# Gate products of one attention stage: thirteen queries in one product, or twelve as two products in the two halves of the TensorE rows

## The chip, the core and the metric

The kernel runs on one core of a Trainium2 chip. The metric is the device time of one execution in microseconds (us). Four compute engines work from queues of their own and in order: PE (TensorE, matrix products into PSUM), DVE (VectorE), ACT (ScalarE) and POOL (GpSimd). SP (SyncE) issues the DMAs. An engine that waits for a semaphore holds up everything behind it in its queue. PSUM has eight banks per partition, each of 512 fp32 numbers. All data here is fp32.

An fp32 matrix product appears in the trace as two passes, each with a weight load (row PEld) and a MATMUL (row PE). A PE transpose is one pass.

## What is computed

The program is a block of two layers: gated cross-attention, a batch attention with a mixture of experts, a second cross-attention and a spiking network. The change concerns the first stage alone, cut here to what it touches:

```
emb  = [sin(mul), cos(mul)],  mul = 100 * log(box relations) * (1, 1000^-1/2)    # per query, key
g    = relu(emb @ Wg.T + bg)                                    # a gate per head, query, key
a    = q @ k.T / sqrt(64)
mn   = softmax(log(clip(g, 1e-6)) + a)
out  = (mn @ v) @ Wo.T + bo
x    = x + tanh(g_xattn[0]) * out
```

There are 8 batches of 512 queries and 512 keys, 16 heads of 64. The gate of a head, a query and a key is a product over 16 features: sines and cosines of box distances in x and y, which depend on the query and the key together, and of box widths and heights, which split into a query factor and a key factor.

## The kernel before

**Tiling.** The stage runs over 32 steps (`NSTEP`), each of 128 queries of one batch against all 512 keys. A step has eight pairs of heads (`p` = 0 to 7). While step `i` does its attention, the gates of step `i + 1` are computed, and the features of steps `i + 2` and `i + 3`.

**Gates (`gate_half`, L436).** The 128 queries are cut into ten blocks of `QB` = 13 (the last has 11). A half is one block with two of the four key tiles: two products that contract over `GR` = 116 rows and give 128 keys by 13 x 16 = 208 gates. The stationary operand is a slice of `emb` (key features), the moving one a slice of `wst` (gate weights, with the query factors written in). The rows are 52 cosine features, 8 products and one bias, a gap, and 52 sine features from row 64. Each half has a PSUM tile `pg` of one bank, of which there are two (`bufs=2`). It is then copied into `gates` by DVE in `p` = 0, 2 and 7, by ACT in the others (L455). A step has 20 halves; `HALVES` says how many belong to each pair.

**Order.** PE, ACT and DVE are in `manual_schedule`: in the loop over steps they run in the order in which the code names the work. For a pair `p` it is: `scores(i, p + 1)`, a half, `weigh(i, p)`, a half, `values(i, p - 1)`, a half, then outputs and features.

- `scores` (L460): two products of 64 rows each, one per head, in the upper and the lower half of the PE rows and each with a bank of its own (`pS`, L469). DVE takes the row maximum (`nm`, L473), then ACT two exponentials (`e`, L476).
- `weigh` (L479): eight transposes of `e` into `pT` (L485), and one DVE instruction that multiplies by the gates (`at`, L487).
- `values` (L492): eight products with `v` into `po` (L505); after every second pair DVE divides (L511, L513).
- `outputs` (L518) transposes the result, `mix` (L530) multiplies it by `Wo` once per step, in `p` = 2 (L536).

**Features.** They live in `lt` and `nt`, on 116 partitions by 5 x 512 numbers, 26 queries per tile. For a later step DVE does `offsets` (`p` = 4, 5), `clip` (6), `turns` (0), `whole`, `rest` (1) and `rest_sizes` (2); ACT does `sizes` (5), `log` (7) and `sines` (2). In `p` = 3 `place` moves them into `emb` with four DMAs (L361), and `load_products` adds the product rows. `load_keys` brings key coordinates once per batch with four DMAs. All of these DMAs are issued from SP, in one queue with the loads of `kT` (L419) and `v` (L425), which are issued three pairs (`kT`) and two pairs (`v`) ahead of their use.

PSUM is full: `pg` 2 banks, `pS` 2, `pT` 2, `po` 1, and 1 for the outputs.

Of the kernel before, what the change touches and what calls it, by code (L numbers as in the profile page):

```python
# [12 lines left out]
F32 = mybir.dt.float32  # L13
# [7 lines left out]
P = 128  # L21
B, S, D = 8, 512, 256
NT = B * S // P
NQ = S // P
# [45 lines left out]
            )  # L70


QB = 13
NB = 10
GR = 64 + 4 * QB
PAIRS = H // 2
MANUAL = {mybir.EngineType.PE, mybir.EngineType.Activation, mybir.EngineType.DVE}

# [194 lines left out]
def gated_cross_attention(cx, a, tg, x1q, d, front):  # L273
# [2 lines left out]

    tc, nc, ident = cx.tc, cx.nc, cx.ident
    NSTEP = B * NQ
    NP = NB // 2
    with ExitStack() as es:  # L280
        cp = es.enter_context(tc.tile_pool(name="xc", bufs=1))
        cx.halfpi = cp.tile([P, 1], F32, name="halfpi")
        nc.gpsimd.memset(cx.halfpi, math.pi / 2)
        crow = cp.tile([P, 1], F32, name="crow")
        wo = cp.tile([P, PAIRS, D], F32, name="wo")
        wst = [cp.tile([P, P * H], F32, name=f"wst{k}") for k in range(2)]
        embs = [cp.tile([P, NP, 2, S], F32, name=f"emb{k}") for k in range(2)]
        for e in embs:
            nc.gpsimd.memset(e, 0.0)
        kd = cp.tile([P, 2, S], F32, name="kd")  # L290
        nc.gpsimd.memset(kd, 0.0)
        qs = cp.tile([P, NSTEP * NP], F32, name="qs")
        qi = cp.tile([P, NSTEP * NP], F32, name="qi")
        lt = cp.tile([P, NP, S], F32, name="lt")
        nt = cp.tile([P, NP, S], F32, name="nt")

        def load_keys(b):
            for r0 in (0, 2 * QB, 64, 64 + 2 * QB):
                nc.sync.dma_start(
                    out=kd[r0 : r0 + 2 * QB, b % 2, :],  # L300
                    in_=d["kc"][2 * b + (1 if r0 % 64 else 0)].partition_broadcast(2 * QB),
                )

        def load_products(j):


            nc.sync.dma_start(
                out=wst[j % 2][4 * QB : 4 * QB + 8, :].rearrange("j (q h) -> j q h", h=H),
                in_=d["qx"][:, j * P : (j + 1) * P, :],
            )  # L310
            if j % NQ < 2:
                nc.sync.dma_start(
                    out=embs[j % 2][4 * QB : 4 * QB + 9].rearrange("j a t k -> j (a t) k"),
                    in_=d["kx"][j // NQ // 4, :, j // NQ % 4 * S : (j // NQ % 4 + 1) * S].unsqueeze(1).to_broadcast([9, NB, S]),
                )

        R = slice(0, GR)

        def offsets(j, t0, t1):
            for t in range(t0, t1):
# [33 lines left out]

        def place(j):

            for src, r0 in ((lt, 0), (nt, 64)):
                for half in range(2):  # L360
                    nc.sync.dma_start(  # L361
                        out=embs[j % 2][r0 : r0 + 4 * QB, :, half, :],
                        in_=src[64 * half : 64 * half + 4 * QB],
                    )

        def features(j, *fns):
            for fn in fns:
                if 0 <= j < NSTEP:
                    fn(j)

        with ExitStack() as pro:
            batch = project_all(cx, a, d, pro)
            bp = pro.enter_context(tc.tile_pool(name="bq", bufs=1))
            box = box_terms(cx, a, d, pro)
            bx = bp.tile([P, NSTEP * NP, 2], F32, name="bx")
            nc.sync.dma_start(out=bx, in_=a["boxq"])
            nc.sync.dma_start(out=crow, in_=a["crow"])
            nc.vector.tensor_tensor(qs, bx[:, :, 0], bx[:, :, 1], ALU.add)
            nc.vector.tensor_scalar(qs, qs, 0.5, None, ALU.mult)
            nc.vector.tensor_tensor(qi, bx[:, :, 1], bx[:, :, 0], ALU.subtract)  # L380
            nc.vector.tensor_scalar(qi, qi, 1.0, None, ALU.add)
            nc.vector.reciprocal(qi, qi)
            for b in range(B):
                xnT = batch(b)
                box(b)
                if b == 0:
                    load_keys(0)

                if b < 4:
                    w, cols = wst[b // 2], slice(b % 2 * 8 * P, (b % 2 + 1) * 8 * P)  # L390
                    nc.gpsimd.tensor_copy(w[0:1, cols][:, 0:1], xnT[0:1, 0, 0:1])
                    nc.sync.dma_start(out=w[0:GR, cols], in_=a["wst"][:, cols])
                if b in (4, 5):
                    w = wo[:, 4 * (b - 4) : 4 * (b - 3), :]
                    nc.gpsimd.tensor_copy(w[0:1, 0, 0:1], xnT[0:1, 0, 0:1])
                    nc.sync.dma_start(out=w, in_=a["woT"][:, 4 * (b - 4) : 4 * (b - 3), :])
                if b == 6:
                    bo = cx.bcast(cp, a["bo"], "bo")
                if b in (1, 3, 5):
                    j = b // 2  # L400
                    offsets(j, 0, NP)
                    features(j, sizes, clip, log)
                if b in (2, 4):
                    j = b // 2 - 1
                    load_products(j)
                    features(j, turns, whole, rest, rest_sizes, sines, place)
# [8 lines left out]
        def load_key(i, p):  # L415
            i, p = i + p // PAIRS, p % PAIRS
            if i < NSTEP:
                kTs[i, p] = wk.tile([P, S], F32, name="kT", tag="kT", bufs=3)
                nc.sync.dma_start(out=kTs[i, p], in_=d["k"][i // NQ, p])  # L419
# [12 lines left out]
        def load_rest(i):  # L432
            xts[i] = wk.tile([P, D], F32, name="xt", tag="xt", bufs=1)
            nc.sync.dma_start(out=xts[i], in_=a["x"][i * P : (i + 1) * P, :])

        def gate_half(i, k, copy):  # L436


            if i == NSTEP:
                return  # L440
            blk, hf = divmod(k, 2)
            if k == 0:
                gates[i] = big.tile([P, H, NQ, P], F32, name="gate", tag="gate")
            q0 = blk * QB
            nq = min(QB, P - q0)
            pg = ps.tile([P, 2, 256], F32, name="pg", tag="g", bufs=2)
            for c in range(2):
                kc = 2 * hf + c
                nc.tensor.matmul(  # L449
                    pg[:, c, 0 : nq * H],  # L450
                    embs[i % 2][R, blk // 2, blk % 2, kc * P : (kc + 1) * P],
                    wst[i % 2][R, q0 * H : (q0 + nq) * H],
                    start=True, stop=True,
                )
            copy(  # L455
                gates[i][:, :, 2 * hf : 2 * hf + 2, q0 : q0 + nq].rearrange("p h k q -> p k h q"),
                pg[:, :, 0 : nq * H].rearrange("p k (q h) -> p k h q", h=H),
            )

        def scores(i, p):  # L460
# [85 lines left out]

        HALVES = (3, 3, 3, 2, 2, 2, 2, 3)
        SINES, LOG = 2, 7  # L550

        for p in range(3):
# [8 lines left out]
        with tc.manual_schedule(engines=MANUAL):  # L561
            for i in range(NSTEP):
                k = 0
                for p in range(PAIRS):
# [4 lines left out]
                    def half():  # L569
                        if halves:  # L570
                            gate_half(i + 1, halves.pop(0), copy)

                    if p == 0:
                        load_queries(i + 1)
                        if (i + 3) % NQ == 0:
                            features(i + 3, lambda j: load_keys(j // NQ))
                    load_key(i, p + 3)
                    scores(i, p + 1)
                    if p == SINES:
                        features(i + 2, rest_sizes, sines)  # L580
                    if p == LOG:
                        features(i + 3, log)
                    half()
                    weigh(i, p)
                    half()
                    values(i, p - 1)
                    load_value(i, p + 2)
                    half()
                    if p in (3, 5, 7):
                        outputs(i, (p - 3) // 2)  # L590
                    if p == 1:
# [8 lines left out]
                        features(i + 2, load_products, place)  # L600
                        load_rest(i)
                    if p == 4:
                        features(i + 3, lambda j: offsets(j, 0, 3))
                    if p == 5:
                        features(i + 3, lambda j: offsets(j, 3, NP), sizes)
                    if p == 6:
                        features(i + 3, clip)
                    if i == NSTEP - 1:
# [1161 lines left out]
def _gate_layouts(boxes, wg, bg):  # L1770


    ntile = B * NQ * (NB // 2)
    boxq = np.zeros((P, ntile, 2), np.float32)
    crow = np.zeros((P, 1), np.float32)
    wst = np.zeros((GR, P, H), np.float32)
    flat = boxes.reshape(B * NQ, P, 4)
    for half in range(2):
        for t in range(NB // 2):
            q = np.minimum(np.arange(QB) + (2 * t + half) * QB, P - 1)  # L1780
            for c in range(2):
                for f in range(2):
                    r0 = 64 * half + (2 * c + f) * QB
                    crow[r0 : r0 + QB] = _turns(f)
                    for e in range(2):
                        boxq[r0 : r0 + QB, t :: NB // 2, e] = flat[:, q, c + 2 * e].T
    for q in range(P):
        for c in range(2):
            for f in range(2):
                r = (2 * c + f) * QB + q % QB  # L1790
                wst[r, q] = wg[:, 2 * c + f]
                wst[64 + r, q] = wg[:, 8 + 2 * c + f]
    wst[4 * QB + 8] = bg

    sc = np.stack([wg[:, 4:8], wg[:, 12:16]]).transpose(2, 0, 1)
    wext = np.stack([sc[:, ::-1], sc])
    return {
        "boxq": boxq,
        "boxc": boxes.reshape(B, S, 2, 2).transpose(0, 3, 2, 1).reshape(2 * B, 2, S),
        "boxt": boxes.reshape(NT, P, 4).transpose(1, 0, 2),  # L1800
        "crow": crow,
        "wst": wst.reshape(GR, P * H),
        "wext": wext.reshape(2 * P),
    }

# [73 lines left out]
```

## Time and profile before

The median of three runs is 2934.63 us (2933.69 to 2938.61). The profiled execution took 2940.68 us, of which the span of the trace is 2938.9 us.

| stretch of the trace, us | PE busy | DVE busy | ACT busy | clock |
|---|---|---|---|---|
| projections, 0 to 354 | 341.13 | 125.06 | 120.42 | 1.00 |
| gates of the first step, 354 to 380 | 22.43 | 8.16 | 9.63 | 1.00 |
| 50 us inside the 32 steps, 1000 to 1050 | 49.83 | 37.38 | 30.31 | 1.00 |
| the rest, 1950 to 2938.9 | 943.39 | 529.43 | 347.24 | 0.96 |

PE busy counts a MATMUL from its start to its modelled end, so passes overlap in it; "idle before" of a group is the time in which its engine had nothing running before an instruction of the group, and the arrow names what ended it. "Clock" is the granted TensorE clock. In the stage of the steps (about 380 to 1950 us) the clock is 1.00 throughout.

### The profile page before, as it was taken

The numbers are of one execution on the slowest core, as the hardware profiler recorded it, in microseconds if no ns is written. First come the engines' busy times: TensorE is split into PE (matmuls) and PEld (weight loads), VectorE is DVE, ScalarE is ACT, GpSimd is POOL, SyncE is SP. The second block draws the span as 40 slices with busy tenths as digits, with TensorE's granted clock in tenths as the row PEclk, the third lists the DMA queues.
The fourth block names the chain that finished last, engine by engine and source line by source line (L and its number), as shares of the span: only waits on it lengthen the run. The fifth ranks groups of instructions, "written<-read, shape, count | busy, mean of one in ns | idle before, by whom it ended". The sixth has DMA issues, their size and how long they took to land.

```text
span 2938.9 us, 39143 instructions
## 1 busy us (share of the span) xinstructions
PE 2866.8 (98%) x15188; PEld 2095.2 (71%) x15188; DVE 1826.5 (62%) x2862; ACT 1404.0 (48%) x2196; POOL 138.4 (5%) x138
## 2 busy tenths in 40 slices
PE   8999999999999999999999999999999998999998
PEld 3444478888888888888888888877775665456566
DVE  6432177777777777777777767557862112566757
ACT  4332256566666666656565665435541121343434
POOL 2000000000000000000000000000002111212100
PEclk9999999999999999999999999999998998999999
DMA  7775545555555555454546464443113333111100
GB/s 226 220 227 188 180 119 155 142 155 142 150 152 146 156 140 158 135 163 131 166 131 167 131 166 129 134 128 140 47 55 129 129 127 107 58 44 57 29 15 22
DMA packets 270105, 381.84 MB, mean 130 GB/s; under 512 B 55048, under 2 KB 136840, under 8 KB 267104
## 3 DMA queue, kind: packets, MB, share of 16 engines
q1 hardware_dynamic: 266848, 370.95, 43.9%
q0 software_dynamic: 3072, 8.39, 1.0%
q8 instruction: 120, 1.97, 0.3%
q14 instruction: 65, 0.53, 0.1%
HBM read 237.23 MB, written 73.88 MB: 106 GB/s over the span
## 4 chain that ended last, share of the span: by engine, by line
PE 79%; DVE 13%; issue 2%; DMA 2%; ACT 1%; SPq 0%; POOL 0%; ACTq 0%; DVEq 0%; POOLq 0%
PE pg L449 13%; PE po L505 11%; PE pS L469 7%; PE pT L485 6%; PE pk L226 6%; PE ph L1525 4%; PE pw L536 4%; PE ph L1308 4%; PE py L1317 4%; PE py L1540 4%; PE pv L241 3%; DVE nm L473 2%; PE pz L1497 2%; DVE lt L346 2%; PE pq L700 2%
## 5 line engine op out<-in xcount | busy, mean ns | idle before, releaser
L476 ACT ACTIVATE e<-pS,nm 128x512 f32<-128x512 f32 x512 | 324.3, 684 | 576.4 <-DVE nm L473 576.0
L449 PE MATMUL pg<-wst,emb 116*128 116x208 f32 (+1 forms) x2560 | 581.5, 350 | 8.1 <-DVE gate L455 5.8
L449 PEld LDWEIGHTS pg<-wst,emb 116*128 116x128 f32 x2560 | 414.1, 189 | 205.2 <-issue 79.8
L505 PEld LDWEIGHTS po<-v,at 128*128 128x128 f32 x4096 | 493.0, 192 | 0.1
L505 PE MATMUL po<-v,at 128*128 128x65 f32 x4096 | 485.7, 272 | 0.0
L473 DVE TENSOR_REDUCE nm<-pS 128x2 f32<-128x1024 f32 x256 | 312.5, 1221 | 176.2 <-PE pS L469 176.2
L487 DVE SCALAR_TENSOR_TENSOR at<-gate,pT 128x1024 f32<-128x1024 f32 x256 | 311.1, 1215 | 46.4 <-PE pT L485 45.4
L469 PE MATMUL pS<-kT,qT 64*128 64x512 f32 x1024 | 291.2, 641 | 5.6 <-ACT e L476 2.0
L485 PE MATMUL pT<-ident,e 128*128 128x128 f32 x2048 | 266.4, 273 | 0.0
L485 PEld LDWEIGHTS pT<-ident,e 128*128 128x128 f32 x2048 | 239.8, 141 | 13.9 <-DVE o L513 1.5
L455 DVE COPY gate<-pg 128x416 f32<-128x416 f32 (+1 forms) x289 | 164.6, 570 | 51.2 <-PE pg L449 30.9
L455 ACT COPY gate<-pg 128x416 f32<-128x416 f32 x351 | 166.7, 531 | 33.6 <-PE pg L449 31.2
L1321 DVE TENSOR_TENSOR ye<-py,b 128x256 f32<-128x256 f32 x32 | 13.6, 424 | 208.0 <-PE py L1317 208.0
L1312 ACT ACTIVATE hT<-ph,eb 128x512 f32<-128x512 f32 x64 | 44.0, 687 | 177.7 <-PE ph L1308 171.9
L226 PE MATMUL pk<-ctxT,wk__121 128*128 128x512 f32 x256 | 114.9, 604 | 11.2 <-DMA ctxT<-in_ctxT 7.6
L63 POOL TENSOR_TENSOR ln_rs<-ln_ve,mhalf 128x4 f32<-128x4 f32 (+1 forms) x25 | 25.5, 1019 | 2050.5 <-DVE ln_ve L62 1990.3
L1525 PE MATMUL ph<-xnT,wf 128*128 128x512 f32 (+2 forms) x320 | 118.7, 513 | 1.8 <-ACT xnT L1393 1.5
L536 PE MATMUL pw<-wo,oT 128*128 128x256 f32 x512 | 117.6, 383 | 0.5 <-ACT oT L528 0.5
L241 PE MATMUL pv<-wv,ctxT 128*128 128x512 f32 x256 | 114.7, 593 | 1.0 <-DVE vs L245 1.0
L1308 PE MATMUL ph<-dT,w 128*128 128x512 f32 x256 | 111.9, 595 | 2.7 <-DVE dT L1293 2.1
L469 PEld LDWEIGHTS pS<-kT,qT 64*128 64x128 f32 x1024 | 77.8, 184 | 51.1 <-issue 36.4
L226 PE MATMUL pk<-xnT,wq 128*128 128x512 f32 x256 | 113.0, 594 | 0.6 <-DVE xnT L261 0.6
(252 smaller groups left out, 3910.7 us busy)
## 6 DMA issues: line engine op xcount, KB each, us to landing
v<-vdr SPq DMA_DIRECT2D x256, 260.0 KB
kT<-kdr SPq DMA_DIRECT2D x256, 256.0 KB
emb<-lt SPq DMA_DIRECT2D x64, 520.0 KB
emb<-nt SPq DMA_DIRECT2D x64, 520.0 KB
vdr<-vs SPq DMA_DIRECT2D x8, 2080.0 KB
kdr<-st SPq DMA_DIRECT2D x64, 256.0 KB
qdr<-st SPq DMA_DIRECT2D x64, 256.0 KB
qT<-qdr SPq DMA_DIRECT2D x32, 512.0 KB
```

Source lines behind the costliest of these rows:

```text
L226: nc.tensor.matmul(pk, w[:, c, m * P : (m + 1) * P], src[:, c, :], start=(c == 0), stop=(c == 1))
L449: nc.tensor.matmul(pg[:, c, 0 : nq * H], embs[i % 2][R, blk // 2, blk % 2, kc * P : (kc + 1) * P], wst[i % 2][R, q0 * H : (q0 + nq) * H], ...
L455: copy(gates[i][:, :, 2 * hf : 2 * hf + 2, q0 : q0 + nq].rearrange("p h k q -> p k h q"), pg[:, :, 0 : nq * H].rearrange("p k (q h) -> p k ...
L469: nc.tensor.matmul(pS[:, t, :], qTs[i][rows, p, :], kT[rows, :], start=True, stop=True)
L473: nc.vector.tensor_reduce(nm, pS, AX.X, ALU.max, negate=True)
L476: nc.scalar.activation(e[:, t, :], pS[:, t, :], AF.Exp, bias=nm[:, t : t + 1])
L485: nc.tensor.transpose(pT[:, t, kc, :], e[:, t, kc * P : (kc + 1) * P], ident)
L487: nc.vector.scalar_tensor_tensor(at, gates[i][:, 2 * p : 2 * p + 2], 1e-6, pT, ALU.max, ALU.mult)
L505: nc.tensor.matmul(po[:, 2 * (p % 2) + t, :], at[:, t, kc, :], v[:, kc, t, :], start=(kc == 0), stop=(kc == NQ - 1),)
L536: nc.tensor.matmul(pw, oT[:, c, :], wo[:, c, :], start=(c == 0), stop=(c == PAIRS - 1))
L1308: nc.tensor.matmul(ph, w1[:, c, f * P : (f + 1) * P], dT[:, c, :], start=(c == 0), stop=(c == 1),)
L1525: nc.tensor.matmul(ph[:, 0:n], wf[:, c, f * P : (f + 1) * P], xnT[:, c, tok], start=(c == 0), stop=(c == 1),)
```

## The change

The block becomes twelve queries: six in rows 0 to 56 of PE and six in rows 64 to 120 (`QB` = 6, `GR` = 57). `g` counts these two row halves: `g` = 0 holds queries 0 to 63 of the step, `g` = 1 queries 64 to 127. A half is now four products of 57 rows and 6 x 16 = 96 columns, in the order c = 0: g = 0, g = 1; c = 1: g = 0, g = 1. There are 11 blocks, so 22 halves in a step; the last block has 4 queries per row half. `pg` is one tile `pgs` of two banks for the whole stage: each row half has its bank, and inside each bank the first 256 columns belong to halves with `hf` = 0, the others to `hf` = 1.

The order in a pair becomes: a half, `scores`, a half, a half, `weigh`, `values`. Features are computed on 128 partitions by 4 x 512 numbers; `place` takes 20 DMAs in place of 4, `load_keys` 12 in place of 4, and `load_products` twice as many.

```diff
-QB = 13
-NB = 10
-GR = 64 + 4 * QB
+HQ = P // 2
+QB = 6
+NB = 11
+GR = 8 * QB + 9
+NS = P // (4 * QB)
...
         def place(j):
...
-            for src, r0 in ((lt, 0), (nt, 64)):
-                for half in range(2):
+            for src, r0 in ((lt, 0), (nt, 4 * QB)):
+                for s in range(NS):
+                    rows = src[4 * QB * s : 4 * QB * (s + 1)]
+                    for g in (s // 2,) if s < 4 else (0, 1):
+                        b0, n = (4 * (s % 2), 4) if s < 4 else (8, 2)
+                        nc.sync.dma_start(
+                            out=embs[j % 2][64 * g + r0 : 64 * g + r0 + 4 * QB, b0 : b0 + n, :],
+                            in_=rows[:, 0:4, :] if s < 4 else rows[:, 2 * g : 2 * g + 2, :],
+                        )
+                for t in range(4):
+                    at = 64 * (t // 2) + r0 + 8 * (t % 2)
                     nc.sync.dma_start(
-                        out=embs[j % 2][r0 : r0 + 4 * QB, :, half, :],
-                        in_=src[64 * half : 64 * half + 4 * QB],
+                        out=embs[j % 2][at : at + 8, NB - 1, :], in_=src[4 * QB * NS :, t, :]
                     )
...
+        pgs = ps.tile([P, 2, 2, 2 * P], F32, name="pg", tag="g")
+
         def gate_half(i, k, copy):
...
-            nq = min(QB, P - q0)
-            pg = ps.tile([P, 2, 256], F32, name="pg", tag="g", bufs=2)
+            nq = min(QB, HQ - q0)
+            pg = pgs[:, :, hf, 0 : 2 * nq * H].rearrange("p g (k n) -> p g k n", k=2)
             for c in range(2):
                 kc = 2 * hf + c
-                nc.tensor.matmul(
-                    pg[:, c, 0 : nq * H],
-                    embs[i % 2][R, blk // 2, blk % 2, kc * P : (kc + 1) * P],
-                    wst[i % 2][R, q0 * H : (q0 + nq) * H],
-                    start=True, stop=True,
-                )
+                for g in range(2):
+                    rows = slice(64 * g, 64 * g + GR)
+                    nc.tensor.matmul(
+                        pg[:, g, c, :],
+                        embs[i % 2][rows, blk, kc * P : (kc + 1) * P],
+                        wst[i % 2][rows, q0 * H : (q0 + nq) * H],
+                        start=True, stop=True,
+                    )
...
-        HALVES = (3, 3, 3, 2, 2, 2, 2, 3)
+        HALVES = (3, 3, 3, 2, 2, 3, 3, 3)
...
                     load_key(i, p + 3)
+                    half()
                     scores(i, p + 1)
                     if p == SINES:
                         features(i + 2, rest_sizes, sines)
                     if p == LOG:
                         features(i + 3, log)
                     half()
+                    half()
                     weigh(i, p)
-                    half()
                     values(i, p - 1)
                     load_value(i, p + 2)
-                    half()
...
                     if p == 4:
-                        features(i + 3, lambda j: offsets(j, 0, 3))
+                        features(i + 3, lambda j: offsets(j, 0, 2))
                     if p == 5:
-                        features(i + 3, lambda j: offsets(j, 3, NP), sizes)
+                        features(i + 3, lambda j: offsets(j, 2, NP), sizes)
```

## The prediction, made before the changed kernel ran

> **What bounds the kernel now.** First the page, then windows, a timeline inside the steps, and the rows of the groups. PE runs without a gap from 380 to 1950 us (49.83 of 50 us busy in the window from 1000), and the chain of waits names PE for most of the span:
>
> ```profile
> PE 79%; DVE 13%; issue 2%; DMA 2%; ACT 1%; SPq 0%; POOL 0%; ACTq 0%; DVEq 0%; POOLq 0%
> ...
> L449 PE MATMUL pg<-wst,emb 116*128 116x208 f32 (+1 forms) x2560 | 581.5, 350 | 8.1 <-DVE gate L455 5.8
> ...
> L738 PE MATMUL pS<-qkT 64*128 64x128 f32 x256 | 23.9, 307 | 0.0
> ```
>
> The gate products wait 8.1 us in all. The third row, from the batch attention, has the form that the change gives them. One pair of heads, p = 6 (columns: start, us, engine, line):
>
> ```profile
> 1009.95 1.13 PE L469 MATMUL pS<-kT,qT 64*128 64x512 f32 x4
> ...
> 1011.01 0.97 PE L449 MATMUL pg<-wst,emb 116*128 116x208 f32 x4
> 1011.19 1.22 DVE L473 TENSOR_REDUCE nm<-pS 128x2 f32<-128x1024 f32 x1 [1.45 <-PE pS L469]
> ...
> 1011.81 1.04 PE L485 MATMUL pT<-ident,e 128*128 128x128 f32 x8
> ...
> 1012.57 1.26 ACT L476 ACTIVATE e<-pS,nm 128x512 f32<-128x512 f32 x2
> ...
> 1012.69 0.87 PE L449 MATMUL pg<-wst,emb 116*128 116x208 f32 x4
> ...
> 1013.39 1.90 PE L505 MATMUL po<-v,at 128*128 128x65 f32 x16
> 1013.70 0.96 ACT L455 COPY gate<-pg 128x416 f32<-128x416 f32 x2
> ```
>
> Read it thus: PE is full, and ACT copies both gate halves only after the exponentials, 2.7 us after the first half starts and 1.0 after the second. That costs nothing, since a half waits for the copy of two halves earlier: each has its own tile. L469 starts the pairs p = 3, 4, 5, 6, 7, 0, 1, 2 at 993.67, 999.17, 1004.45, 1009.95, 1015.22, 1021.26, 1027.30, 1033.55, and p = 3 again at 1043.42: a step is 49.75 us.
>
> **What the change takes off PE.** Starts of single passes: a gate pass comes each 0.175 us, so 18 halves of 4 passes (0.70) and two narrower (0.59) are 13.8 us a step. In L738, passes of the two row halves start 7 ns apart, and a pair of passes each 0.107 to 0.112, the same as L505 with 65 columns: a pass costs its weight load there, so 96 columns won't beat it. A new half, four pairs of passes, is 0.44; 22 are 9.6. **PE saves 4.2 us a step.** Were the row halves not concurrent: 19.2, a loss of 5.4.
>
> Other edits. DVE feature rows sum to 11.5 us a step (L324 5 x 0.54; L333 1.48, L339 1.54, L342 1.49, L346 2.82, L82 1.48): a fifth, 2.3, goes; of ACT's four at 2.34, 1.9 goes. ACT gains two copies (+1.0). All lies beside PE, except where it stands before a copy (below). Copies of 384 instead of 416 numbers: 0.50 ACT, 0.55 DVE. `place`: 4 issues of 0.87 become 20 of some 0.33 (estimate, as kT's 0.32 to 0.43), +3.1 us on SP; the queued kT and v loads are over 9 us ahead of use, which hides it; uncovered it would cost 3 us a step. `load_keys` has 8 more issues per batch: under 1 us a step, same cover. Switches between whole-row and half-row products (0.2 us between passes instead of 0.11) stay at two a pair.
>
> **The wait it adds.** `pgs` holds both halves in the same two banks. In the program as built, each half waits for the copy of the half just before it; in the old one, of two before. The Trainium skill ("PSUM — Partial Sum Buffer", section "PSUM bank collisions raise a hardware error") says to guard PSUM by bank, not by address, as an engine reading a bank collides with PE writing elsewhere in it. So this wait belongs to the layout: by address two halves are free and 4.2 us are gained; by bank there is one buffer. No run here shows a collision; the waits in the program decide.
>
> And the new order puts halves B and C together behind the scores. Walk p = 6, t = 0 where half A starts on PE:
> - A 0 to 0.54 (first weight load exposed, 0.11, as in L738); results 0.75. Copy A on ACT 2.2 to 2.7 (behind `sizes`); pS 0.54 to 1.40.
> - nm starts 1.13 after pS starts (trace above, less the switch): 1.67 to 2.89. Exponentials 2.93 to 4.19, behind copy A.
> - B may start at 2.75; copy B stands behind the exponentials on ACT: 4.2 to 4.73. **C waits for it: 4.78 to 5.32.**
> - Queued behind C on PE: transposes 5.42 to 6.40, `values` to 8.19, next A at 8.3. Before: 5.27.
>
> The same for each pair, PE at clock 1.00, then at 0.50 (every PE duration doubled, DVE and ACT unchanged):
>
> | p | before | clock 1.00 | clock 0.50 | what ends the wait |
> |---|---|---|---|---|
> | 3 | 5.50 | 6.05 | 9.8 | next A: copy B behind table load and exponentials |
> | 4 | 5.28 | 4.80 | 9.4 | none |
> | 5 | 5.50 | 8.7 | 13.4 | C: copy B behind exponentials; nm 0.2 late behind offsets |
> | 6 | 5.27 | 8.3 | 13.0 | as walked |
> | 7 | 6.04 | 8.1 | 12.2 | B: copy A behind clip (to 2.5); C: copy B behind nm (4.3) |
> | 0 | 6.04 | 7.0 | 11.7 | C: copy B behind nm (3.5) |
> | 1 | 6.25 | 8.9 | 13.4 | C: as p = 6, nm 0.4 late behind turns |
> | 2 | 9.87 | 13.3 | 18.1 | B: copy A behind whole and rest (3.2); C: copy B behind nm, rest_sizes (6.2) |
> | sum | 49.75 | 65.15 | 101.0 | |
>
> At clock 1.00 a step costs +15.4; 31 steps have halves: +477. The first step's 22 halves stand alone: each 0.75 to the copy, 0.53 copy, 0.05: 1.33, 29 us plus scores, against 23.6: +7. Sum on the profiled run: 2940.7 + 484 = **3425**.
>
> **The clock.** C's wait leaves PE idle for up to 2.9 us in a row. Here is what idling did to the clock elsewhere in this trace (window, us, PE busy, PEld, DVE, ACT, POOL, clock):
>
> ```profile
> 1974.61:1978.02 3.41, 1.53 (x16) 1.17 (x14) 3.31 (x6) 0.10 (x1) 0.00 (x0) 1.00 0.53 150
> 1978.02:1981.43 3.41, 2.97 (x13) 1.91 (x14) 2.03 (x10) 3.09 (x11) 1.01 (x1) 0.50 0.78 90
> ...
> 2216.95:2220.37 3.42, 3.42 (x18) 3.42 (x17) 0.25 (x1) 0.00 (x0) 0.00 (x0) 0.50 0.00 0
> ```
>
> 1.53 us busy in a stretch of 3.41, and the next stretch is at half clock; and at 2216.95 passes of 32 columns, back to back, do not bring it back. I counted, per stretch of 3.41 us (the grid on which the clock changes), the share in which columns stream (0.83 ns a column of a product, half that for a transpose): the clock fell after stretches with 0.00 to 0.29 (eight; one of 0.26 kept it; all others at full clock had 0.35 or more), stayed low up to 0.75, and rose from 0.82 on. The Trainium skill ("TensorE: Matmul & The Clock Gate", section "HAM oscillation — how this bites in real kernels") asks only for no idle gap above some 3.4 us. By that rule 2.9 us are harmless and the sum stays 3425. By the rows, a stretch that begins 0.75 to 3.5 us into p = 5, 6 or 1 streams under 0.29: 2.75 of 3.41, 80% of phases. I take the rows.
>
> At low clock a pair streams about half its time (`values` 65 of 128 columns' time), too little to rise, until `mix` in p = 2 (6.9 us of full streaming). So p = 3 and 4 run at full clock, p = 5 falls near its end (11.5), p = 6, 7, 0, 1 are low, and in p = 2 mix ends at full clock: 6.05 + 4.80 + 11.5 + 13.0 + 12.2 + 11.7 + 13.4 + 18.1 = 90.8. With a fifth of the falls one pair late and a short rise now and then: 88. 31 x (88 - 49.75) = 1186, the first step +10: 2940.7 + 1196 = 4137 for the profiled run. The median lies 6 us lower: **4130**.
>
> **Rivals.**
> - Clock stays up: 3425. For it: no idle gap reaches 3.4 us; against: the windows above. 0.17.
> - Falls, but rises often in p = 7 or 0: 3500 to 3850. 0.15.
> - Faster: the waits hide, and PE keeps its 4.2 us: 2940 - 31 x 4.2 = 2810. It needs all waits of a step under 4.2 us, 0.5 at each C; a copy alone is 0.5. For it: DVE is idle for a quarter of the step, ACT for two fifths; against: their order is fixed, and it puts the exponentials before copy B. 0.04.
> - Smaller waits than walked: 2945 to 3300. 0.04.
> - Row halves run one after the other: up to 0.44 more per half, +300 at full clock; inside the range with the forecast. L738 speaks against.
>
> The forecast has 0.60, with 3850 to 4350 as its own range. 3380 to 4350 adds the middle case and half of the first rival: about 0.8. 0.2% (6 us) is what a measurement can tell from no change: faster 0.04, same 0.01, slower 0.95.
>
> **What shows it.** The pg group (5632 passes) has hundreds of us idle before it, ended by gate copies of both engines; B to C apart by exponentials or nm; pass pairs 0.11 apart at clock 1.00; clock digits of 5 to 8 in the steps' slices. Wrong if the group's idle stays near 8 us, or the clock at 9.

## The result, and the profile after

The changed kernel takes **3879.78 us** (median of four runs, 3875.76 to 3896.08) against 2936.62 us for the kernel before in the same comparison: a ratio of **1.3218**, interval 1.3173 to 1.3264. The profiled execution took 3882.64 us, its span is 3880.9 us, and the mean granted clock is 0.807.

The first view is again the page: the chain of waits, the row of the gate products, and the row of the scores, which wait for keys.

```profile
PE 68%; DVE 12%; ACT 5%; SPq 4%; issue 2%; DMA 2%; POOL 0%; DVEq 0%; ACTq 0%; POOLq 0%
...
L468 PE MATMUL pg<-wst,emb 57*128 57x96 f32 x5632 | 605.5, 347 | 424.4 <-ACT gate L474 272.8
...
L489 PE MATMUL pS<-kT,qT 64*128 64x512 f32 x1024 | 364.4, 793 | 13.1 <-DMA kT<-kdr 12.5
```

The gate products now wait 424.4 us (8.1 before), mostly for copies by ACT. Their busy time (the time in which at least one of their passes runs) did not fall (605.5 against 581.5 us), although a pass has 96 columns in place of 208. The 942.0 us that the span has gained divide on PE like this: PE busy went from 2866.8 to 3378.7 us (+511.9), and PE idle from 72.1 to 502.2 us (+430.1), of which the gate products are 416.3.

The timeline of one pair, p = 5 (columns: start, us, engine, line), shows both:

```profile
1079.39 0.69 PE L468 MATMUL pg<-wst,emb 57*128 57x96 f32 x8
...
1079.91 1.05 PE L489 MATMUL pS<-kT,qT 64*128 64x512 f32 x4
...
1080.80 0.59 PE L468 MATMUL pg<-wst,emb 57*128 57x96 f32 x8
...
1081.31 1.22 DVE L493 TENSOR_REDUCE nm<-pS 128x2 f32<-128x1024 f32 x1
1082.56 1.27 ACT L496 ACTIVATE e<-pS,nm 128x512 f32<-128x512 f32 x2 [1.96 <-DVE nm L493]
1083.72 0.48 ACT L474 COPY gate<-pg 128x384 f32<-128x384 f32 x1
...
1084.25 1.17 PE L468 MATMUL pg<-wst,emb 57*128 57x96 f32 x8 [2.86 <-ACT gate L474]
...
1085.35 1.97 PE L505 MATMUL pT<-ident,e 128*128 128x128 f32 x8
...
1087.11 3.51 PE L525 MATMUL po<-v,at 128*128 128x65 f32 x16
```

The three L468 rows are halves A, B and C. B is done at 1081.4, but its copy stands on ACT behind `nm` and both exponentials; C starts 2.86 us late. C's own eight passes then take 1.17 us where A's took 0.69, the transposes 1.97 (1.04 before), the values 3.51 (1.90 before): that is the clock at half. The windows of the same stretch (us, then busy time of PE, PEld, DVE, ACT, POOL, then clock, DMA share, GB/s) show when it went:

```profile
1076.83:1080.25 3.42, 3.42 (x34) 3.24 (x34) 2.62 (x4) 1.77 (x4) 0.00 (x0) 1.00 0.27 74
1080.25:1083.66 3.41, 1.13 (x12) 0.56 (x8) 2.14 (x3) 1.45 (x3) 0.00 (x0) 1.00 0.59 130
1083.66:1087.07 3.41, 2.82 (x16) 2.65 (x17) 0.00 (x0) 1.02 (x3) 0.00 (x0) 0.50 0.68 173
...
1090.49:1093.90 3.41, 3.41 (x17) 1.70 (x18) 0.00 (x0) 2.58 (x3) 0.00 (x0) 0.50 0.89 261
1093.90:1097.31 3.41, 0.91 (x16) 0.74 (x16) 1.23 (x1) 1.64 (x3) 0.00 (x0) 1.00 0.78 251
```

The stretch with C's wait holds 1.13 us of PE work, and the next one is at 0.50. At 1093.90 the clock is back for one stretch, and the wait for copy B of p = 6 takes it away again.

Where the 942 us lie along the run, by the starts of the gate and mix passes: up to the first gate product +10.8, gates of the first step +20.9 (44.0 against 23.1), the 32 steps **+913.4** (2496.8 against 1583.3), everything behind them -3.2. The clock over the steps' stretch is 0.72, behind it 0.97 (0.96 before).

### The profile page after: what moved, and what is told of

Same layout as the page of the kernel before. It is cut to its first block, busy times and chain, and to the rows that moved or that the text cites. A ratio compares the mean times of both kernels' runs of the same rounds, so it can differ in the third digit from the quotient of the medians.

```text
span 3880.9 us, 46550 instructions
## 1 busy us (share of the span) xinstructions
PE 3378.7 (87%) x18260; PEld 2524.8 (65%) x18260; DVE 1777.4 (46%) x2831; ACT 1385.9 (36%) x2259; POOL 139.3 (4%) x137
## 4 chain that ended last, share of the span: by engine, by line
PE 68%; DVE 12%; ACT 5%; SPq 4%; issue 2%; DMA 2%; POOL 0%; DVEq 0%; ACTq 0%; POOLq 0%
PE po L525 14%; PE pg L468 9%; PE pT L505 8%; PE pS L489 7%; DVE nm L493 6%; PE pw L556 4%; ACT e L496 3%; PE ph L1545 3%; PE ph L1328 3%; PE py L1337 3%; PE py L1560 3%; SPq L371 2%; PE pk L228 2%; PE pz L1517 1%; SPq L377 1%
## 5 line engine op out<-in xcount | busy, mean ns | idle before, releaser
L468 PE MATMUL pg<-wst,emb 57*128 57x96 f32 x5632 | 605.5, 347 | 424.4 <-ACT gate L474 272.8
L468 PEld LDWEIGHTS pg<-wst,emb 57*128 57x128 f32 x5632 | 511.6, 245 | 710.8 <-ACT gate L474 396.7
L525 PEld LDWEIGHTS po<-v,at 128*128 128x128 f32 x4096 | 699.5, 265 | 0.1
L525 PE MATMUL po<-v,at 128*128 128x65 f32 x4096 | 697.9, 343 | 0.0
L505 PE MATMUL pT<-ident,e 128*128 128x128 f32 x2048 | 403.5, 360 | 0.0
L474 ACT COPY gate<-pg 128x384 f32<-128x384 f32 x414 | 199.2, 481 | 494.8 <-PE pg L468 492.4
L489 PE MATMUL pS<-kT,qT 64*128 64x512 f32 x1024 | 364.4, 793 | 13.1 <-DMA kT<-kdr 12.5
L505 PEld LDWEIGHTS pT<-ident,e 128*128 128x128 f32 x2048 | 318.1, 184 | 36.1 <-issue 18.5
L474 DVE COPY gate<-pg 128x384 f32<-128x384 f32 (+1 forms) x290 | 152.4, 525 | 235.8 <-PE pg L468 235.8
L556 PEld LDWEIGHTS pw<-wo,oT 128*128 128x128 f32 x512 | 131.8, 265 | 26.4 <-ACT oT L548 0.7
```

The costliest lines, as they stand in the source:

```text
L468: nc.tensor.matmul(pg[:, g, c, :], embs[i % 2][rows, blk, kc * P : (kc + 1) * P], wst[i % 2][rows, q0 * H : (q0 + nq) * H], start=True, st ...
L474: copy(gates[i][:, :, 2 * hf : 2 * hf + 2, :] .rearrange("p h k (g q) -> p g k h q", g=2)[:, :, :, :, q0 : q0 + nq], pg.rearrange("p g k ( ...
L489: nc.tensor.matmul(pS[:, t, :], qTs[i][rows, p, :], kT[rows, :], start=True, stop=True)
L505: nc.tensor.transpose(pT[:, t, kc, :], e[:, t, kc * P : (kc + 1) * P], ident)
L525: nc.tensor.matmul(po[:, 2 * (p % 2) + t, :], at[:, t, kc, :], v[:, kc, t, :], start=(kc == 0), stop=(kc == NQ - 1),)
L556: nc.tensor.matmul(pw, oT[:, c, :], wo[:, c, :], start=(c == 0), stop=(c == PAIRS - 1))
```

## The experiments

Two theories: the shared banks and the copy's place behind the exponentials make PE wait, and the waits lower the clock (the forecast's); or the loss comes from something else in the change: the row halves, the order of the pair, or `place` with its twenty DMAs. Each ratio is to the kernel before in the same comparison (2937.8 to 2938.8 us).

### One row half alone, with a buffer each

Gates of queries 64 to 127 are not computed; each half has its own bank, two in turn, as in the kernel before.

```diff
-        pgs = ps.tile([P, 2, 2, 2 * P], F32, name="pg", tag="g")
...
+            pgt = ps.tile([P, 512], F32, name="pg", tag="g", bufs=2)
...
-                for g in range(2):
+                for g in range(1):
```

> The order, the copies and the features of the changed kernel, but only the products of row half 0 are done (the gates of queries 64 to 127 are left out; each copy reads the same 192 numbers twice), and each half has a bank of its own, two in turn. The pitch of the passes stays that of the weight load, so PE has the same time to fill. Theory 'one buffer' (both halves lie in the same two banks, so a half waits for the copy of the half just before): the waits go, idle before the gate products falls from 424 us to under 40, the clock stays above 0.97 and the time is near 2940 - 31 x 4.2 = 2810 (2770 to 2900). Rival 'order' (the new place of the halves, all in front of the transposes, is what stalls PE): waits stay, over 3300. Rival 'half rows' (57-row products keep the clock low by themselves): no waits but a clock under 0.9, over 3200.

Measured: 3690.24 us, ratio 1.2559 (1.2397 to 1.2721), clock 0.78. A miss: 880 us above the expected 2810. The gates' wait did go (27.7 us in the 96-column products, 389.7 in the changed kernel), but the timeline from p = 5 into p = 6 shows what stood behind it:

```profile
1030.00 4.87 SPq L371 DMA_DIRECT2D emb<-nt  x6
...
1034.91 2.67 SPq L377 DMA_DIRECT2D emb<-nt  x4
...
1038.12 0.42 SPq L434 DMA_DIRECT2D kT<-kdr  x1
...
1040.91 2.08 PE L488 MATMUL pS<-kT,qT 64*128 64x512 f32 x4 [6.28 <-DMA kT<-kdr]
```

SP is still issuing `place` (L371, L377) when a quick step needs its next keys; `kT` is issued at 1038.12, and PE waits 6.28 us, once per step, 194.0 us in all. After it the four score passes take 2.08 us: half clock again. Such a wait does not keep the clock at 0.78 by itself: with both row halves, a kernel further down waits 202 us for keys in the same way, at a clock of 0.94. What else is slow here comes up with the second version of this kernel.

### The order of the pair

First, the order of the kernel before, with the shared banks of the change (`scores`, a half, `weigh`, a half, `values`, a half):

```diff
-                    half()
                     scores(i, p + 1)
...
-                    half()
                     weigh(i, p)
+                    half()
                     values(i, p - 1)
                     load_value(i, p + 2)
+                    half()
```

> The changed kernel with the old order of a pair (scores, half, transposes, half, values, half); the shared banks stay. 'One buffer': half 2 waits for copy 1, which ACT does behind the exponentials, but PE has the transposes in between, so 1.6 us of wait a pair are left instead of 2.9, and idle stretches are too short to lower the clock often: about 3300 (3150 to 3500), clock above 0.9. Rival 'order': 2800 to 2950, as the old order is back.

Measured: 3706.03 us, ratio 1.2613 (1.257 to 1.2656), clock 0.85; gates wait 318 us. Setting the order back recovers 174 of 943 us. The order is a small part of the cause, and the waits with one buffer cost more than expected in either order (the time is 206 us above the range).

Then only the queue on ACT is changed: `exponents` split off from `scores` and named behind half B, so that copy B runs before the exponentials.

```diff
                     scores(i, p + 1)
+                    half()
+                    exponents(i, p + 1)
...
                     half()
-                    half()
                     weigh(i, p)
```

> The changed kernel, with one thing moved on ACT: the two exponentials come behind the copy of the second half instead of in front of it. Banks and order of PE stay. 'One buffer' with the queue on ACT as what makes the wait long: in the pairs with ACT copies C waits 0.7 us (latency and copy) instead of 2.9; the pairs with DVE copies keep theirs (copy B behind the row maximum). Steps near 56 us, time about 3140 (3000 to 3300), clock above 0.95. If the exponentials were not what holds the copy: unchanged, 3880.

Measured: 3545.98 us, ratio 1.2068 (1.1907 to 1.2229), clock 0.88. 334 us come from the place of the exponentials alone; the range was missed by 246 us. Groups of this kernel by line and shape:

```profile
L468 PE MATMUL pg<-wst,emb 57*128 57x96 f32 x5120 | 481.2, 312 | 189.3 <-DVE gate L474 128.0 <-ACT gate L474 60.4 <-issue 0.9
L489 PE MATMUL pS<-kT,qT 64*128 64x512 f32 x1024 | 335.6, 733 | 166.6 <-DMA kT<-kdr 164.6 <-DMA v<-vdr 1.5 <-ACT e L503 0.5
```

The gates' wait for ACT fell from 272.3 to 60.4 us, and the keys' wait rose from 12.5 to 164.6: the same `place` in SP's queue.

### Filling the wait

To part the wait from the clock, PE gets useless work where it waits: four products of 64 x 512 between B and C, their result overwritten, in pairs with three halves.

```diff
                     half()
+                    if halves and i + 1 < NSTEP:
+                        fill(i)
                     half()
```

> The changed kernel with work added: in each pair of three halves PE does four more products of 64 rows by 512 columns between half B and half C (1.7 us at full clock, into the transposes' banks, overwritten by them; the results are not used). 'Idle lowers the clock': they fill the wait, the clock stays above 0.95 and the time falls to that of the walk at clock 1.00, 3350 to 3430, though PE does 27 us... 31 x 6 x 1.7 = 316 us more work. Rival 'the clock is low for another reason' (half-row products, few columns): clock stays near 0.8, 3880 or more.

Measured: **3508.33 us**, ratio 1.194 (1.1878 to 1.2002), 80 us above the top of the expectation, and 371 us *faster* than the changed kernel. The group of the added products:

```profile
L506 PE MATMUL pT<-qT,ident 64*128 64x512 f32 x1488 | 423.9, 694 | 0.0
```

PE runs these products for 423.9 us (the time in which at least one of them runs), and the mean clock is 0.952 instead of 0.807. The eight transposes of a pair take 1.09 us again. This run shows that PE's low clock in the changed kernel is due to its idling, not to the products in row halves as such.

### `place` by itself

The kernel before, with nothing changed but `place` cut into twenty DMAs:

```diff
-                    nc.sync.dma_start(
-                        out=embs[j % 2][r0 : r0 + 4 * QB, :, half, :],
-                        in_=src[64 * half : 64 * half + 4 * QB],
-                    )
+                    for t in range(NP):
+                        nc.sync.dma_start(
+                            out=embs[j % 2][r0 : r0 + 4 * QB, t, half, :],
+                            in_=src[64 * half : 64 * half + 4 * QB, t, :],
+                        )
```

> The kernel before, with place alone changed: the same bytes in 20 DMAs instead of 4. 'Two waits': SP is held some 11 us longer, the kT load of pair 7 comes about 6 us late in each step, PE stands still and the clock falls for some pairs: 3100 to 3500. Rival 'hidden' (my prediction's line: kT and v are loaded over 9 us ahead, so nothing is lost): 2935 to 2950.

Measured: 3102.9 us, ratio 1.0559 (1.0534 to 1.0584). The listing of the DMA's line (ns, smallest, median, largest) and the groups:

```profile
L362 SPq DMA_DIRECT2D emb<-lt x320: 743/755/1547, 75.3 to 2010.0; - x160
L362 SPq DMA_DIRECT2D emb<-nt x320: 743/744/1515, 113.1 to 2017.9; - x160
```

```profile
L470 PE MATMUL pS<-kT,qT 64*128 64x512 f32 x1024 | 311.4, 681 | 102.6 <-DMA kT<-kdr 100.5 <-ACT e L477 2.0
```

An issue costs SP 0.74 us, twenty 14.8, and PE waits 100.5 us for keys. So `place` in twenty DMAs costs 164 us by itself (these are not quite the twenty of the change: each has 52 rows of 2 KB).

In the changed kernel the same cost is nearly covered. There `place` was issued in two parts, `lt` in p = 3 and `nt` in p = 6:

```diff
-                        features(i + 2, load_products, place)
+                        features(i + 2, load_products, lambda j: place(j, (0,)))
...
+                        features(i + 2, lambda j: place(j, (1,)))
                         features(i + 3, clip)
```

> The changed kernel with place in two parts and nothing else. 'Two waits': in the changed kernel steps are 75 us long, kT waits only 12.5 us in all, so place costs little there: 3750 to 3900. If place were a main cause of the loss there too: under 3500.

Measured: 3838.02 us, ratio 1.306 (1.3034 to 1.3086): 42 us. The same split in the kernel with one row half (again without the gates of queries 64 to 127):

> As e1 (products of row half 0 alone, a bank for each half, gates of queries 64 to 127 left out), but the twenty DMAs of place are issued in two parts: the ten of lt after pair 3, the ten of nt after pair 6. In e1 the gate waits were gone, yet each step stood 6.3 us for a kT load that SP issued behind 14.8 us of place, and the clock stayed at half until mix. Theory 'two waits' (shared banks, and behind them place on SP): without both, PE is full at 1.00, steps of 45 to 47 us, time 2780 to 2900, clock above 0.95. If e1 was slow for another reason (half-row products hold the clock down): over 3300, clock under 0.9.

Measured: 3351.26 us, ratio 1.1404 (1.1352 to 1.1455), clock 0.83. 339 us faster than without the split, yet 450 above the expectation: the wait moves once more, to DVE, whose `offsets` for the step after wait 66.2 us for the DMAs of `place` that still read `lt`. Why the clock stays that low was not tried by a run of its own, but the traces of the two kernels with one row half narrow it down. Count for each stretch of 3.41 us the share in which columns stream, as the prediction did, but with transposes in full (why in full is told further down). The clock then rose after 32 of 170 low stretches with a share from 0.80 on in the first of these kernels, and after 38 of 134 in the second. With the gate products of the single row half counted at a quarter, it rose after 32 of 32 and 38 of 38. So products in one row half alone seem to do little to bring the clock back.

### Two buffers for both row halves

PSUM has no two banks more. But `pT` (two banks) lives only between the transposes and `at`: halves and `pT` can share two tiles of two banks. The whole computation, with exponentials behind copy B, `place` in two parts, and in every pair copies A and B on ACT and copy C on DVE:

```diff
-            pg = pgs[:, :, hf, 0 : 2 * nq * H].rearrange("p g (k n) -> p g k n", k=2)
+            pgt = ps.tile([P, 2, 4 * P], F32, name="pg", tag="g", bufs=2)
+            pg = pgt[:, :, 0 : 2 * nq * H].rearrange("p g (k n) -> p g k n", k=2)
...
-            pT = ps.tile([P, 2, NQ, P], F32, name="pT", tag="t")
+            pTt = ps.tile([P, 2, 4 * P], F32, name="pT", tag="g", bufs=2)
+            pT = pTt.rearrange("p t (k q) -> p t k q", k=NQ)
...
                     scores(i, p + 1)
+                    half()
+                    exponents(i, p + 1)
...
-                    half()
-                    half()
+                    half(nc.vector.tensor_copy)
                     weigh(i, p)
```

> The whole computation. The gate tile of a half and the transposes' tile share one pair of two-bank buffers in turn, so that a half waits for the copy of two halves before; the exponentials come behind the copy of half B on ACT, the third copy is on DVE; place in two parts as in e5. 'Two waits': no long wait is left; PE saves up to 4.2 us a step; 2800 to 2930 and clock above 0.95, at or under the kernel before. If concurrent row halves were themselves slow: over 3200.

Measured: **2976.61 us**, ratio 1.0155 (1.0106 to 1.0204), clock 0.956: 861 us below the changed kernel with the same split of `place`. The time is 47 us above the expected range; `offsets` wait 73.6 us for `place`, as above. Three variants of this kernel take its parts to pieces. With `place` whole, on SP:

> As e6, with place in one piece on SP after pair 3. 'Two waits': once the banks no longer hold PE up, place does: the kT load of pair 7 comes 5 to 7 us late in each step and the clock falls: 3150 to 3500 against 2977 in e6. If place were hidden: 2980.

Measured: 3133.52 us, ratio 1.0664 (1.0642 to 1.0685), 17 us under the expectation; keys wait 202.2 us. `place` whole, but issued from POOL (`nc.gpsimd`) at the start of p = 3:

> As e6 (two two-bank buffers in turn for gate halves and transposes, exponentials behind copy B), with all twenty DMAs of place issued from POOL, which is idle in this stage, as soon as the sines are done. In e6 DVE waited 73.6 us for lt to be free (29 waits, up to 7.8 us), the kT loads no longer. Theory 'two waits': with place off SP, steps come near 45.5 to 47 us: 2800 to 2890, clock above 0.97, under the kernel before. Rival 'POOL is slower at issuing than SP': offsets wait longer, 2980 to 3150.

Measured: 2956.12 us, ratio 1.0038 (1.0006 to 1.007); a miss, and level with the kernel before. The rows of the scores in these two, `place` on SP first:

```profile
L488 PE MATMUL pS<-kT,qT 64*128 64x512 f32 x1024 | 306.5, 674 | 202.7 <-DMA kT<-kdr 202.2 <-ACT e L502 0.5
L488 PE MATMUL pS<-kT,qT 64*128 64x512 f32 x1024 | 290.8, 642 | 4.5 <-DMA kT<-kdr 3.5 <-ACT e L502 0.5
```

So `place` on SP costs this kernel 177 us. The timeline of p = 6 with `place` on POOL:

```profile
1040.06 1.91 ACT L337 ACTIVATE lt<-lt 128x2048 f32<-128x2048 f32 x1 [0.98 <-DVE lt L331]
...
1041.87 0.84 ACT L473 COPY gate<-pg 128x384 f32<-128x384 f32 x2
1042.39 0.69 PE L467 MATMUL pg<-wst,emb 57*128 57x96 f32 x8 [1.97 <-ACT gate L473]
...
1044.05 3.52 PE L532 MATMUL po<-v,at 128*128 128x65 f32 x16
```

`sizes` (L337) stands on ACT before the copies of A and B; C waits 1.97 us; the values run at half clock. The same kernel with the exponentials put back before copy B:

> As e9, with the exponentials back in front of copy B on ACT. The transposes take the buffer of half B, so they wait for copy B: 2.3 us a pair in PE. 'One buffer': the second buffer helps only when the copy is not behind the exponentials: steps of 58 to 62 us, 3250 to 3500. If the buffer alone were enough: within 2% of e9.

Measured: 3185.15 us, ratio 1.0839 (1.0818 to 1.0861), 65 us under the expected range. The second buffer alone is not enough:

```profile
L512 PE MATMUL pT<-ident,e 128*128 128x128 f32 x2048 | 296.9, 291 | 236.4 <-DVE gate L473 140.2 <-ACT gate L473 96.2
L467 PE MATMUL pg<-wst,emb 57*128 57x96 f32 x5120 | 404.1, 285 | 31.1 <-ACT gate L473 30.1 <-issue 0.9
```

The wait passes from C to the transposes, but mostly not to where the expectation had it. By what each of them waits for, and by the banks in the built program, the transposes take the buffer of half C in p = 0, 1, 5, 6 and 7, and wait there 0.7 to 1.2 us for its copy, which stands on DVE behind `nm` (140.2 us). Only in p = 2 do they take that of half B and wait 3.1 us for its copy behind the exponentials on ACT (96.2). So two buffers with the exponentials in front are slow, but a wait of 2.3 us for copy B in each pair is not what was measured.

### A version under both

In the variant that issues from POOL, `sizes` moves behind the exponentials of p = 6, and in p = 0 (whose copy A stands behind `log`) DVE copies half A.

```diff
-                    half()
+                    half(nc.vector.tensor_copy if p == 0 else nc.scalar.copy)
                     scores(i, p + 1)
...
                     exponents(i, p + 1)
+                    if p == 6:
+                        features(i + 3, sizes)
...
-                        features(i + 3, lambda j: offsets(j, 2, NP), sizes)
+                        features(i + 3, lambda j: offsets(j, 2, NP))
```

> e9_rotating_pool with its two remaining waits of gate halves for ACT taken away: sizes (1.91 us on ACT) moves from the end of p = 5 to p = 6 behind the exponentials, so that the copies of halves A and B of p = 6 no longer stand behind it (wait 1.97, then half clock through p = 6: 9.4 us for the pair), and in p = 0 the copy of half A is made by DVE, not by ACT behind log (wait 0.88). Theory (what is left of the loss in e9 is these two waits and the clock they lower): p = 6 takes about 5.2 us and p = 0 about 5.4, a step about 45.5 us against some 51 on average, clock 0.97 or more: 2780 to 2870 us, under before. Rival (other copies behind other work on ACT and DVE take their place, as they did in e6 and e9): 2900 to 2970.

Measured: **2860.59 us** (2856.88 to 2869.49), ratio **0.9738** (0.972 to 0.9756), clock 0.978. Faster than the kernel before by 2.6%. The page's busy row and two groups:

```profile
PE 2743.4 (96%) x18260; PEld 2022.5 (71%) x18260; DVE 1729.6 (60%) x2769; ACT 1423.8 (50%) x2321; POOL 461.9 (16%) x777
...
L467 PE MATMUL pg<-wst,emb 57*128 57x96 f32 x5632 | 423.4, 282 | 5.7 <-DVE gate L473 2.6
...
L512 PE MATMUL pT<-ident,e 128*128 128x128 f32 x2048 | 281.5, 281 | 35.9 <-ACT gate L473 22.1
```

PE runs the same 18260 matmuls as in the changed kernel, in 2743.4 us instead of 3378.7: most of the difference, 635 us, is likely the clock (0.978 against 0.807), since the instructions are as many; how passes overlap differs a little too. A step is 46.6 us (49.75 before), and the 32 steps are 97.7 us shorter; up to the first gate product the run is 17.1 us longer, which was not traced further.

| what was varied | us | gate wait on PE, us | clock |
|---|---|---|---|
| the change | 3879.78 | 424 | 0.81 |
| copy B before the exponentials | 3545.98 | 228 | 0.88 |
| wait filled with PE work | 3508.33 | 193 | 0.95 |
| two buffers, copy B behind the exponentials, `place` on POOL | 3185.15 | 31 (transposes 236) | 0.95 |
| two buffers, copy B first, `place` on SP | 3133.52 | 33 (keys 202) | 0.94 |
| two buffers, copy B first, `place` on POOL | 2956.12 | 65 | 0.96 |
| and the last two copies moved | 2860.59 | 6 | 0.98 |

## Why the prediction was right, and where it was off

**Slower, by waits and clock: right.** The forecast, 4130 us, lies 250 us (6%) above the measurement, which is in the forecast's own range. That it is in this range is in part luck: 3880 is 30 us from its end, and the split of `place` showed 42 us of a cost that the forecast had put at nothing; without them the time is 3838, below the range. The rivals with the clock up (3425) and with small waits fell; so did "faster", for the layout as changed.

**The wait behind copy B: right in place and size.** Walked: PE idle for up to 2.9 us in a row before C. In the trace of p = 5: 2.86. Over all steps the wait before C is 2.64 to 2.92 us in p = 5, and 2.2 us on average in p = 6. That it takes both one buffer and ACT's order is shown by the kernels that change one of them. With copy B first and `place` on SP, the second buffer takes 3546 us to 3134 (which engine copies which half changes with it). With two buffers and `place` on POOL, the exponentials in front of copy B take 2956 us to 3185.

**The clock: right that it falls, and after what.** The prediction weighed the rows of the trace against the Trainium skill ("TensorE: Matmul & The Clock Gate", section "HAM oscillation — how this bites in real kernels"), which asks only for no idle gap above some 3.4 us. Here the clock fell in p = 5 in all 31 steps, with no gap before C longer than 2.92 us, and work put into the gaps brought its mean from 0.807 to 0.952: the rows were the better guide.

**How long it stays low: the mis-sized term.** The forecast had the clock low from the end of p = 5 until `mix`, 90.8 us a step and 88 with an allowance; the trace gives 79.5. In 31 steps that is 264 us too much, which with 11 us too little for the first step makes up the difference of 250. By pairs, over all steps:

| p | walked, clock 1.00 / 0.50 | forecast | measured mean | mean clock |
|---|---|---|---|---|
| 3 | 6.05 / 9.8 | 6.05 | 5.88 | 1.00 |
| 4 | 4.80 / 9.4 | 4.80 | 4.68 | 1.00 |
| 5 | 8.7 / 13.4 | 11.5 | 10.71 | 0.76 |
| 6 | 8.3 / 13.0 | 13.0 | 11.81 | 0.66 |
| 7 | 8.1 / 12.2 | 12.2 | 9.76 | 0.67 |
| 0 | 7.0 / 11.7 | 11.7 | 8.48 | 0.78 |
| 1 | 8.9 / 13.4 | 13.4 | 11.07 | 0.73 |
| 2 | 13.3 / 18.1 | 18.1 | 16.91 | 0.60 |

Where a pair ran wholly at one clock, the walk is 0.1 to 0.9 us too long (p = 7: 7.44 and 11.27; p = 0: 6.74 and 11.03). The larger part is the clock: p = 0 was wholly at full clock in 15 of 31 steps and p = 7 in 7, where the forecast had none. The rival "rises often in p = 7 or 0" named just this, and the result is 30 us above its end. The rule behind it, that the clock stays low up to a share of 0.75, held for the stretches of the trace before but not here: counted the same way, the clock rose after 33 of 178 low stretches with a share of 0.5 to 0.6. Many of these hold all of a pair's transposes, which the count took at half. Counted in full, transposes make the stretches part: the clock rose after none of 223 low stretches with a share under 0.70, 42 of 146 up to 0.80, and 69 of 70 above. Over the twelve traces of this case in which no row half runs alone, it rose after 1 of 1016, 180 of 486 and 477 of 501. So the half weight of the transposes is the likely error; it is a count over kept traces, and no run was made for it.

**PE saves 4.2 us a step: about right.** Passes of the two row halves start 7 ns apart, and at full clock a pair of passes comes every 0.109 to 0.112 us. In the version without waits the gate products are busy for 423.4 us instead of 581.5, 4.9 us in each of 32 steps; that version keeps 3.1 us a step of it.

**`place` hidden, +3.1 us on SP: wrong, and covered up.** Its twenty issues take 0.74 us (L371) and 0.64 (L377), 14 us a step, not 6.6 from the estimate of 0.33, and 9 us of lead do not hide 14. In the changed kernel keys wait only 12.5 us in all, since a step of 79 us gives SP time; with steps of some 50 us it costs 164 us (the kernel before with twenty DMAs) or 177 (two buffers). The two costs are not a sum: the larger wait hides the smaller.

**First step, +10: off by a factor of two** (+20.9); its gates wait alone at a clock of 0.62. It is a small term.

Not tried: two halves in one bank, told apart by address and without the wait.

## What to carry to other kernels

When products in two row groups have a bank each, as here, the same number of banks gives half as many buffers: count the buffers first, and read which copy each product then waits for, and what stands ahead of that copy in its engine's queue. A wait on PE can cost more than twice its length (against the last version, with as many products, the change has 387 us more idling on PE and 635 us more busy time), because here the clock fell after the waits and stayed low until a stretch of dense work. And when an experiment removes the largest wait and the time hardly moves, look for the next resource that the slow step had been covering.

## What was not expected of the hardware

- A DMA from SBUF to SBUF holds SP for 0.74 us with 24 rows of 4 or 8 KB and for 0.64 with 8 rows of 2 KB, against 0.32 to 0.43 for a load of `kT`. In the kernel before 52 rows of 10 KB take 0.87, and cut into 2 KB each 0.74. From POOL's queue the issue takes 0.50 (L371 in the last version).
- More work on PE made the program 371 us faster (0.952 against 0.807 of the clock).
- The clock by stretches of 3.41 us in the changed kernel, by the share in which columns stream, with transposes at half: it fell after 100 of 100 stretches under 0.25, 5 of 10 up to 0.30, 6 of 37 up to 0.40, and none above; it rose after 62 of 63 from 0.8 on, 14 of 31 from 0.7 to 0.8, 33 of 178 from 0.5 to 0.6, and 1 of 122 under 0.5. With transposes in full, over the twelve traces in which no row half runs alone, it fell after 647 of 682 stretches under 0.40, 23 of 228 up to 0.45, and none of 8666 above.
